# Graph attention behind an expert layer: where the head weights are made ready, and node terms as columns of the head products

## The chip, the cores and the metric

The kernel runs on one core of a Trainium2 chip. The metric is the device time of one execution in microseconds, from start to end, with the median over several executions. The kernel is a long chain of eight layers that hand one 256x768 feature matrix to each other; this text looks at the seam between the sixth (experts, called L2 ffn) and the seventh (graph attention, called L3 gnn).

## The reference

Before the seam comes a mixture of eight experts with top-2 routing, plus one shared expert. Behind it, after a layer norm, stands this graph attention with 12 heads of 64 features (here for 256 nodes and 4096 edges):

```
hv  = h.reshape(n, 12, 64)
ft  = einsum('nhd,od->nho', hv, W)              # one 64x64 weight for all heads
a1  = sum(ft * attn_l, -1);  a2 = sum(ft * attn_r, -1)      # two terms per node and head
e   = leaky_relu(a1[src] + a2[dst], 0.2)
w   = exp(e - segment_max(e, dst)[dst])
agg = segment_sum(w / segment_sum(w, dst)[dst] * ft[src], dst)
res = einsum('nhd,od->nho', hv, W_res)
out = relu(agg + res)
```

A last attention layer with low-rank experts (L3 ffn) follows.

## The kernel before

The 256 rows are two chunks of 128 partitions (`NC = 2`), and the 768 features are six slices of 128 (`KD = 6`). A feature-major copy `xT` of the normed input (`turn_chunk`, line 171 transposes on TensorE, line 172 copies on ScalarE) feeds the products.

**Order of work.** Engines run their queues in order. A planner decides at build time in which order instructions stand in each queue, by modelled costs and dependences; it may move a load or a vector operation far ahead of its place in the text. Instructions wrapped in `pin` keep the order of the text among themselves on their engine. Tiles come from pools with a fixed number of buffers; a new tile of a name waits until the oldest one's readers are done.

**L2 ffn (pools `f2`, `f2a`).** After the router and two thirds of the shared expert, six expert tiles of 128 routed rows are worked off (`for u, parts in enumerate(TILES2)`, line 1695). For each, `pick` (line 1193, VectorE) prepares a one-hot, `take` gathers the rows of a tile ahead with an indirect DMA on the GpSimd queue (line 1120, tile `xg`, buffers `rows`, four of them), `up_tile` and `down_tile` multiply (line 1153), `gated` (lines 1651 to 1657, VectorE) forms the activation, and the result goes to DRAM from the ScalarE queue (line 1210). Weights are streamed by the SP queue through a ring of eight buffers. After the last tile, `add_rows` gathers four times 128 rows back (`yg`, also in the `rows` buffers) and adds them (line 1169); `end_tiles` adds the last products (line 1370) and norms each chunk into `xn` (lines 150 to 160).

**L3 gnn (pools `g3`, `g3a`).** The head weight `W` stands twice on the diagonal of a 128x128 tile, so that one product serves two heads; `bd` holds this for `W` and for `W_res`. It is cleared on VectorE (line 1726), and four DMAs of the ScalarE queue fill its diagonal blocks (line 1729). From `bd` and the two attention rows, VectorE forms `own` (lines 1738 and 1740): `W` applied to the attention vectors, four columns for each pair of heads. Then:

- line 1748: 24 small products `ps_a2 = xT . own`, four columns wide, and line 1751 copies them into `a2`, the node terms `a1` and `a2` of the reference;
- line 1767 (`spread`): products with one column of `own` as broadcast weight, which put a source term on all partitions;
- line 1761 (`piece`): the head products `ft` and `res`, six slices for each of the two chunks, copied out by ScalarE (line 1763). There are four such pieces; two ride behind each of the first two spreads;
- `gat`: for each pair of heads and each chunk, in a software pipeline, `leaky` (line 298 on ScalarE with `a2` as bias, line 299 on VectorE), the row maximum (line 305), the exponentials (line 311), the counted sums (line 318), a transpose (line 326) and the weighted sum (line 338). All of it is pinned.

Attention rows are loaded by `row`, on the GpSimd queue, into a pool of five; the planner issues these loads early (the two of this layer at 999.3 and 1006.8 us). The tile tagged `wide` is a single buffer of 2048 floats per partition, used in turn for `xn` and for the one-hots `hot` of `find` (line 1099). `cnt1` is a mask of the second graph layer; its first half is used again for `mixT` in the expert layers.

Of the kernel before, what the change touches and what calls it, by code (L numbers as in the profile page):

```python
# [8 lines left out]
F32 = mybir.dt.float32  # L9
# [4 lines left out]
OP = mybir.AluOpType  # L14
AX = mybir.AxisListType
# [3 lines left out]
P = 128  # L19
N = 256  # L20
NC = 2
D = 768
KD = D // P
# [30 lines left out]
def graph_ffn_stack_kernel(ctx: ExitStack, tc: tile.TileContext, a: dict, out: bass.AP):  # L54
    nc = tc.nc
# [21 lines left out]
    def acc2(name="acc"):  # L77
        return psacc.tile([P, 2, 512], F32, tag="acc", name=name)
# [18 lines left out]
    pin = tc.keep_in_program_order  # L97
# [16 lines left out]
    def halves(t):  # L114
        return t.rearrange("p (a n) -> p a n", a=2)
# [320 lines left out]
    with tc.tile_pool(name="g0", bufs=1) as g0, tc.tile_pool(name="g0t", bufs=2) as g0t, \  # L436
# [35 lines left out]
        pieces = [(r, c, i) for r in range(NREL) for c in range(NC) for i in range(2)]  # L472

        with tc.tile_pool(name="graph", bufs=1) as gp, tc.tile_pool(name="onehot", bufs=5) as oh:
# [14 lines left out]
            for e in range(NE // P):  # L489
# [31 lines left out]
            ps = bank("ps_cnt").rearrange("p (d n) -> p d n", d=NC)  # L521
# [190 lines left out]
        for layer in range(2):  # L712
# [114 lines left out]
    def wide(name):  # L827
        return masks.tile([P, 2048], F32, tag="wide", name=name)
# [4 lines left out]
    def row(name):  # L833
        src = a[name]
        t = rows.tile([P, 1024], F32, tag="row", name="row")[:, :src.shape[0]]
        nc.gpsimd.dma_start(t, src.partition_broadcast(P))
        return t
# [350 lines left out]
    def pick(pool, is_e, parts):  # L1188

        t = pool.tile([72, P], BF16, name="own")  # L1190
        at = 0
        for r, _, n in parts:
            nc.vector.tensor_copy(t[:, at:at + n], is_e[:, r:r + 1].to_broadcast([72, n]))
            at += n
        return t
# [335 lines left out]
            ready=lambda h: dots(g2a, a2, xl2, 1, 1, D, (asrc, adst), (0,)))  # L1531


    with tc.tile_pool(name="f2", bufs=1) as f2, tc.tile_pool(name="f2a", bufs=2) as f2a:
        table = held.tile([N, D], F32, name="table2")
        nc.gpsimd.dma_start(table.rearrange("(c p) d -> p c d", p=P), xn)
# [76 lines left out]
        more = plan(TILES2)[3]  # L1613

        def gathered(name):
            return f2a.tile([P, D], F32, tag="rows", name=name, bufs=4)

        ys = results[1]

# [72 lines left out]
        cwT = weights_t(f2, cw, 9, "cwT2")  # L1692
        xgT = tile_t(f2a, xg, "xgT")
        last = None
        for u, parts in enumerate(TILES2):
            own, now = pick(f2a, is_e, parts), xgT
            if u < end:
                xg = take(slots[:, u + 1:u + 2])
            acc = acc2("up1_acc")
            up_tile(acc, now, parts, 0, own, range(6), u)  # L1700
            h = first_factor(acc)
            if last is not None:
                gT = turned(f2a, last)
            if u < end:
                xgT = tile_t(f2a, xg, "xgT")
            acc = acc2("up3_acc")
            up_tile(acc, now, parts, 1, own, range(3), u)
            if last is not None:
                finish(f2a, ys[u - 1], gT, views(TILES2[u - 1], "2"), TILES2[u - 1])
                free(u - 1, "2")  # L1710
            up_tile(acc, now, parts, 1, own, range(3, 6), u)
            last = gated(acc, h)
# [9 lines left out]


    with tc.tile_pool(name="g3", bufs=1) as g3, tc.tile_pool(name="g3a", bufs=2) as g3a:
        bd = g3.tile([P, 2, P], F32, name="bd")
        nc.vector.memset(bd, 0.0)
        for i, n in enumerate(("L3_gnn_WT", "L3_gnn_WresT")):
            for j in range(2):
                nc.scalar.dma_start(bd[j * 64:(j + 1) * 64, i, j * 64:(j + 1) * 64], a[n])

        own = g3.tile([P, KD, 2, 2], F32, name="own3")
        nc.vector.memset(own, 0.0)
        for i, n in enumerate(("L3_gnn_attn_l", "L3_gnn_attn_r")):
            r = row(n)
            for j in range(2):
                js = slice(j * 64, (j + 1) * 64)
                t = g3a.tile([P, KD, 64], F32, name="of_row")
                nc.vector.tensor_tensor(t[js], r.rearrange("p (k j o) -> p j k o", k=KD, j=2)[js, j],
                                        bd[js, 0, None, js].to_broadcast([64, KD, 64]), OP.mult)
                nc.vector.tensor_reduce(own[js, :, i, j], t[js], AX.X, OP.add)  # L1740
        xT = g3.tile([P, KD, N], F32, name="xT5")
        for c in range(NC):
            turn_chunk(xn, xT, KD, c)
        a2 = st([P, 2, NC, 12], "gat_a12")
        ps = bank("ps_a2")
        for c in range(NC):
            for k in range(KD):
                nc.tensor.matmul(ps[:, c * 24 + k * 4:c * 24 + k * 4 + 4], xT[:, k, c * P:(c + 1) * P],
                                 own[:, k].rearrange("p w j -> p (w j)"), start=True, stop=True)
        for w in range(2):  # L1750
            nc.vector.tensor_copy(a2[:, w].rearrange("p c (k j) -> p c k j", k=KD),
                                  ps[:, :48].rearrange("p (c k w j) -> p w c k j", c=NC, k=KD, w=2)[:, w])
        ft = g3.tile([P, NC, D], F32, name="ft")
        res = g3.tile([P, NC, D], F32, name="res")
        pieces = [(i, c) for i in range(2) for c in range(NC)]

        def piece():
            i, c = pieces.pop(0)
            acc = acc2("ft_acc")
            for k in range(KD):  # L1760
                pin(nc.tensor.matmul(acc[:, k // 3, (k % 3) * P:(k % 3 + 1) * P], xT[:, k, c * P:(c + 1) * P],  # L1761
                                     bd[:, i, :], start=True, stop=True))
            pin(nc.scalar.copy(halves((ft, res)[i][:, c, :]), acc[:, :, :384]))

        def spread(h, w, ps):
            for j in range(w):
                pin(nc.tensor.matmul(ps[:, j, :], own[:, h // 2, 0, j:j + 1].to_broadcast([P, P]), xT[:, h // 2, :],
                                     start=True, stop=True))
            for _ in range(2 if pieces else 0):
                piece()  # L1770

        h = g3.tile([P, NC, D], F32, name="h5")
        last_xn = normed()

        def post(d, hs, acc, rs):
            scaled(h, acc, rs, 64, 12, hs, d, res[:, d, :])
            s = slice(hs[0] * 64, (hs[-1] + 1) * 64)
            nc.vector.scalar_tensor_tensor(x[:, d, s], h[:, d, s], 0.0, x[:, d, s], op0=OP.max, op1=OP.add)
            if hs[-1] == 11:
                norm(x, last_xn, D, d)  # L1780

        gat(g3a, ft, 12, 64, a2, cnt, neg, OP.max, post, True, spread=spread)
        xn = last_xn

# [134 lines left out]
```

## Time and profile before

| | |
|---|---|
| three runs | 1452.01, 1454.04, 1456.68 us, median 1454.04 us |
| the profiled execution | 1456.74 us, span 1455.0 us |
| TensorE busy | 1259.4 us (87%), mean granted clock 0.916 |
| VectorE, ScalarE, GpSimd busy | 670.2, 477.0, 356.3 us |
| the expert tiles of L2 ffn | about 1107 to 1233 us of the span |
| end of L2 ffn, norm | about 1233 to 1258.6 us |
| L3 gnn up to the pipeline's second leaky | about 1257.9 to 1282 us |
| L3 gnn, rest | about 1282 to 1333 us |
| L3 ffn | from there to 1455 us |

The stage windows of a profile give busy time for each engine in a stretch of the span, and behind it the clock granted to TensorE (1.00 is full speed), the busy share of the DMA engines and what they moved. The chain of waits follows the end of the program back: each line is a start, a duration and the engine and line that held the chain for that time; "ACTq" is ScalarE's queue issuing DMAs, and "issue" is time for which the profile names no wait. A record of a product in this trace is one pass; a product in single precision has two.

### The profile page before, as it was taken

What the parts mean: (1) busy time and instruction counts of PE and PEld (TensorE: products, weight loads), DVE (VectorE), ACT (ScalarE), POOL (GpSimd) and SP (SyncE); (2) the same over time, 40 slices, a digit from 0 to 9 for tenths busy, and PEclk for the clock granted to TensorE, in tenths of its full rate; (3) what the DMA queues carried; (4) which work ended last, traced back from release to release, by engine and by line L of the source; (5) the groups of instructions that cost most, each with busy time, mean ns of one, the idle gap of its engine ahead of it and who ended that gap; (6) DMA issues with size and microseconds to landing.
All of it is one profiled execution on the core that took longest, in us unless ns stands there. A gap on an engine that the chain in (4) does not pass through costs nothing. (4 is left out here: it accounts for less than half of the span.)

```text
span 1455.0 us, 13968 instructions
## 1 busy us (share of the span) xinstructions
PE 1259.4 (87%) x5081; PEld 775.6 (53%) x5102; DVE 670.2 (46%) x1273; ACT 477.0 (33%) x825; POOL 356.3 (24%) x194
## 2 busy tenths in 40 slices
PE   7999999789997874998989859866889999777998
PEld 4576444347643432854545445435576554466854
DVE  4421999930099996164352530067351011455023
ACT  1013877611287662241231122215221111163122
POOL 1001999800099991000203010111001000100000
PEclk9999999989999995999999969987989999775989
DMA  9323250215230023223732149922018998600000
GB/s 332 130 94 102 59 160 6 98 33 195 101 95 0 3 95 115 89 111 143 259 116 76 66 171 389 335 89 73 22 72 342 364 383 334 264 1 33 33 0 22
DMA packets 77689, 196.74 MB, mean 135 GB/s; under 512 B 9036, under 2 KB 23952, under 8 KB 77488
## 3 DMA queue, kind: packets, MB, share of 16 engines
q1 hardware_dynamic: 69088, 162.28, 31.2%
q0 software_dynamic: 6352, 28.33, 5.5%
q10 hardware_dynamic: 2176, 5.18, 1.0%
q8 instruction: 43, 0.70, 0.2%
q14 instruction: 30, 0.25, 0.1%
HBM read 177.45 MB, written 14.87 MB: 132 GB/s over the span
## 5 line engine op out<-in xcount | busy, mean ns | idle before, releaser
L784 POOL TENSOR_TENSOR gate<-gate,qT 128x2048 f32<-128x2048 f32 x64 | 287.8, 4535 | 242.4 <-ACT gate L764 242.0
L769 DVE TENSOR_REDUCE qiT<-gate 128x32 f32<-128x2048 f32 x96 | 215.0, 2279 | 16.2 <-POOL gate L784 15.2
L764 ACT ACTIVATE gate<-gate_acc,bg 128x1024 f32<-128x1024 f32 x192 | 209.8, 1114 | 38.1 <-PE gate_acc L760 35.5
L759 PE MATMUL gate_acc<-sela,ga 128*128 128x512 bf16 x363 | 139.2, 384 | 25.3 <-ACT gate L764 24.8
L760 PE MATMUL gate_acc<-selb,gb 112*128 112x512 bf16 x384 | 147.8, 385 | 1.2
L1153 PE MATMUL up_acc<-w_e,xgT 128*64 128x384 f32 (+1 forms) x432 | 96.4, 489 | 0.0
L760 PEld LDWEIGHTS <-gb 112*128 112x128 bf16 x384 | 37.6, 98 | 96.4 <-issue 71.5
L791 DVE TENSOR_TENSOR gate<-gate,ps_qy 128x2048 f32<-128x2048 f32 x32 | 72.9, 2278 | 0.2 <-ACT gate L764 0.2
L1153 PEld LDWEIGHTS up_acc<-w_e,xgT 128*64 128x64 f32 (+1 forms) x432 | 46.9, 154 | 44.7 <-issue 27.3
L759 PEld LDWEIGHTS <-ga 128*128 128x128 bf16 x384 | 37.8, 98 | 47.8 <-issue 2.2
L642 PE MATMUL ps_alpha<-w_qb,qiT 128*128 128x384 f32 x96 | 44.1, 553 | 19.8 <-DVE qiT L769 19.8
L566 DVE TENSOR_TENSOR ps_hg<-ps_hg,hg 128x384 f32<-128x384 f32 x8 | 4.5, 563 | 107.9 <-ACT hg L565 107.9
L326 PE MATMUL ps_pt<-ident,gat_z 128*128 128x128 f32 x104 | 23.8, 366 | 33.6 <-DVE gat_s L318 33.5
L1120 POOL DMA_INDIRECT yg<-ys,rows x8 | 7.6, 953 | 177.3 <-DMA w_a<-in_L_ffn_AT 118.6
L171 PE MATMUL ps_tr<-ident,xn 128*128 128x128 f32 x84 | 17.7, 380 | 35.4 <-DVE xn L160 20.3
L267 DVE CUSTOM_DVE_ANT_0 gat_dot<-xl,row 128x128 f32<-128x128 f32 (+2 forms) x56 | 23.8, 425 | 52.8 <-ACT xl L1520 19.6
L457 PE MATMUL ps_z<-w_rel,xT 128*128 128x384 f32 x144 | 47.9, 486 | 0.0
L457 PE MATMUL ps_z<-w_rel,nT 128*128 128x384 f32 x144 | 47.7, 491 | 0.0
L461 ACT COPY z<-ps_z 128x384 f32<-128x384 f32 x24 | 11.5, 479 | 105.0 <-PE ps_z L457 105.0
L1651 DVE TENSOR_TENSOR h<-up_acc,h 128x768 f32<-128x768 f32 x6 | 5.7, 958 | 80.1 <-PE up_acc L1153 80.1
L627 PE MATMUL ps_alpha<-w_qa,gT 128*128 128x384 f32 x96 | 40.1, 499 | 0.0
L338 PE MATMUL gat_acc<-xl,gat_pt 128*128 128x128 f32 (+2 forms) x128 | 34.9, 431 | 5.3 <-DVE gat_s L347 5.3
(444 smaller groups left out, 2192.7 us busy)
## 6 DMA issues: line engine op xcount, KB each, us to landing
w_e<-in_L_ffn_W SPq DMA_DIRECT2D x32, 1152.0 KB, 12.2
w_rel<-in_L_gnn_W_rel SPq DMA_DIRECT2D x12, 1152.0 KB, 8.3
wi<-in_L_ffn_WiT SPq DMA_DIRECT2D x8, 1152.0 KB, 15.0
wo<-in_L_ffn_WoT SPq DMA_DIRECT2D x8, 1152.0 KB, 15.5
w_down<-in_L_ffn_W SPq DMA_DIRECT2D x8, 1152.0 KB, 12.2
w_root<-in_L_gnn_W_root SPq DMA_DIRECT2D x4, 1152.0 KB, 11.1
w_ga<-in_L_gnn_WgAT SPq DMA_DIRECT2D x4, 1152.0 KB, 6.4
w_qa<-in_L_gnn_WqAT SPq DMA_DIRECT2D x4, 1152.0 KB, 5.7
```

The source lines that it names most:

```text
L267: pin(nc.vector.tensor_tensor_reduce(t, xl[:, c, h * C:(h + 1) * C], r[:, h * C:(h + 1) * C], 1.0, 0.0, OP.mult, OP.add, accum_out=a2[:, w ...
L338: pin(nc.tensor.matmul(accs[d][:, i, at:at + wide], pts[h, d][:, j, s, :], xl[:, s, lo:lo + wide], start=s == 0, stop=s == NC - 1))
L457: mm = nc.tensor.matmul(ps, hT[:, k, c * P:(c + 1) * P], w(k, i * 384, (i + 1) * 384), start=k == 0, stop=k == KD - 1)
L627: pin(nc.tensor.matmul(al_ps[c][i], hT[:, k, c * P:(c + 1) * P], w(k, i * 384, (i + 1) * 384), start=k == 0, stop=False))
L642: pin(nc.tensor.matmul(al_ps[c][i], qiT[:, f, c * P:(c + 1) * P], w(f, i * 384, (i + 1) * 384), start=False, stop=f == KD - 1))
L759: pin(nc.tensor.matmul(acc[:, i, :], ga[:, b, fs], sela, start=True, stop=False))
L760: pin(nc.tensor.matmul(acc[:, i, :], gb[0:112, u, b, fs], selb[0:112, i], start=False, stop=True))
L764: pin(nc.scalar.activation(g[:, u * 16:(u + 1) * 16, :].rearrange("p n l -> p (n l)"), acc.rearrange("p a n -> p (a n)"), AF.Sigmoid, bias ...
L769: pin(nc.vector.tensor_reduce(qiT[:, f, b * NPB:(b + 1) * NPB], g, AX.X, OP.add))
L784: pin(nc.gpsimd.tensor_tensor(g, g, q[:, None, :].to_broadcast([P, NPB, LQ]), OP.mult))
L791: pin(nc.vector.tensor_tensor(g, g, q_ps[:, None, :].to_broadcast([P, NPB, LQ]), OP.mult))
L1153: pin(nc.tensor.matmul(ps[at:at + n, :], xT[:, k, at:at + n], ws[r](k, lo, hi), start=start, stop=stop))
```

## The change

The head weights are made ready inside the expert layer, and the node terms come out of the head products.

- A tile `heads3` (128 x 6 x 132) in a pool of its own holds for each slice the doubled `W` on the diagonal (128 columns) and behind it the four columns that were `own`. `res3`, the doubled `W_res`, lies in the second half of `cnt1`.
- Before expert tile 1, the GpSimd queue clears both tiles and loads the diagonal blocks (`diagonal`): two DMAs into `heads3`, each of 64 partitions and six runs of 256 bytes, and two into `res3`. Before tile 2, VectorE forms the four columns (`rows_of_heads`), with `wide` as scratch. These instructions are not pinned.
- The buffers `rows` go from four to three.
- In L3 gnn, `heads_of(c)` multiplies a chunk with all 132 columns per slice; two vector copies take the node terms out of PSUM, one scalar copy the 128 others. `heads_of(0)` stands before the pipeline; `heads_of(1)` and `residual_of(0)` follow the first spread, `residual_of(1)` the second.

```diff
+    heads3 = ctx.enter_context(tc.tile_pool(name="late", bufs=1)).tile([P, KD, P + 4], F32, name="heads3")
+    def diagonal(t, name):
+        for j in range(2):
+            js = slice(j * 64, (j + 1) * 64)
+            if len(t.shape) == 3:
+                nc.gpsimd.dma_start(t[js, :, js], a[name][:, None, :].to_broadcast([64, t.shape[1], 64]))
+            else:
+                nc.gpsimd.dma_start(t[js, js], a[name])
+    def rows_of_heads():
+        for i, n in enumerate(("L3_gnn_attn_l", "L3_gnn_attn_r")):
+            r = row(n)
+            for j in range(2):
+                js = slice(j * 64, (j + 1) * 64)
+                t = wide("of_row")[:, :KD * 64].rearrange("p (k o) -> p k o", k=KD)
+                nc.vector.tensor_tensor(t[js], r.rearrange("p (k j o) -> p j k o", k=KD, j=2)[js, j], heads3[js, :, js], OP.mult)
+                nc.vector.tensor_reduce(heads3[js, :, P + 2 * i + j], t[js], AX.X, OP.add)
...
-            return f2a.tile([P, D], F32, tag="rows", name=name, bufs=4)
+            return f2a.tile([P, D], F32, tag="rows", name=name, bufs=3)
...
+        res3 = cnt1[:, 1, :P]
         for u, parts in enumerate(TILES2):
+            if u == 1:
+                for t, n in ((heads3, "L3_gnn_WT"), (res3, "L3_gnn_WresT")):
+                    nc.gpsimd.memset(t, 0.0)
+                    diagonal(t, n)
+            elif u == 2:
+                rows_of_heads()
...
-        bd = g3.tile([P, 2, P], F32, name="bd")
-        nc.vector.memset(bd, 0.0)
...
-                nc.scalar.dma_start(bd[j * 64:(j + 1) * 64, i, j * 64:(j + 1) * 64], a[n])
-        own = g3.tile([P, KD, 2, 2], F32, name="own3")
...
-        for c in range(NC):
-            for k in range(KD):
-                nc.tensor.matmul(ps[:, c * 24 + k * 4:c * 24 + k * 4 + 4], xT[:, k, c * P:(c + 1) * P],
-                                 own[:, k].rearrange("p w j -> p (w j)"), start=True, stop=True)
...
+        def heads_of(c):
             acc = acc2("ft_acc")
             for k in range(KD):
+                pin(nc.tensor.matmul(acc[:, k // 3, (k % 3) * (P + 4):(k % 3 + 1) * (P + 4)], xT[:, k, c * P:(c + 1) * P],
+                                     heads3[:, k, :], start=True, stop=True))
+            v = acc[:, :, :3 * (P + 4)].rearrange("p i (k f) -> p i k f", k=3)
+            for w in range(2):
+                pin(nc.vector.tensor_copy(a2[:, w, c, :].rearrange("p (i k j) -> p i k j", i=2, k=3),
+                                          v[:, :, :, P + 2 * w:P + 2 * w + 2]))
+            pin(nc.scalar.copy(ft[:, c, :].rearrange("p (i k f) -> p i k f", i=2, k=3), v[:, :, :, :P]))
...
+        heads_of(0)
+        pieces = [(heads_of, 1), (residual_of, 0), (residual_of, 1)]
```

More of the change, by code (lines that the diff above doesn't have):

```diff
@@ L1724, in graph_ffn_stack_kernel @@
     with tc.tile_pool(name="g3", bufs=1) as g3, tc.tile_pool(name="g3a", bufs=2) as g3a:
-        bd = g3.tile([P, 2, P], F32, name="bd")
-        nc.vector.memset(bd, 0.0)
-        for i, n in enumerate(("L3_gnn_WT", "L3_gnn_WresT")):
-            for j in range(2):
-                nc.scalar.dma_start(bd[j * 64:(j + 1) * 64, i, j * 64:(j + 1) * 64], a[n])
-        own = g3.tile([P, KD, 2, 2], F32, name="own3")
[L1732 to L1740, printed above, removed]
         xT = g3.tile([P, KD, N], F32, name="xT5")
@@ L1744, in graph_ffn_stack_kernel @@
         a2 = st([P, 2, NC, 12], "gat_a12")
-        ps = bank("ps_a2")
-        for c in range(NC):
-            for k in range(KD):
-                nc.tensor.matmul(ps[:, c * 24 + k * 4:c * 24 + k * 4 + 4], xT[:, k, c * P:(c + 1) * P],
-                                 own[:, k].rearrange("p w j -> p (w j)"), start=True, stop=True)
-        for w in range(2):
-            nc.vector.tensor_copy(a2[:, w].rearrange("p c (k j) -> p c k j", k=KD),
-                                  ps[:, :48].rearrange("p (c k w j) -> p w c k j", c=NC, k=KD, w=2)[:, w])
@@ L1753, in graph_ffn_stack_kernel @@
         ft = g3.tile([P, NC, D], F32, name="ft")
         res = g3.tile([P, NC, D], F32, name="res")
-        pieces = [(i, c) for i in range(2) for c in range(NC)]
-        def piece():
-            i, c = pieces.pop(0)
+        def heads_of(c):
             acc = acc2("ft_acc")
             for k in range(KD):
+                pin(nc.tensor.matmul(acc[:, k // 3, (k % 3) * (P + 4):(k % 3 + 1) * (P + 4)], xT[:, k, c * P:(c + 1) * P],
[5 more added lines that the diff above has]
+            pin(nc.scalar.copy(ft[:, c, :].rearrange("p (i k f) -> p i k f", i=2, k=3), v[:, :, :, :P]))
@@ L1761, in piece, with residual_of @@
+        def residual_of(c):
+            acc = acc2("res_acc")
+            for k in range(KD):
                 pin(nc.tensor.matmul(acc[:, k // 3, (k % 3) * P:(k % 3 + 1) * P], xT[:, k, c * P:(c + 1) * P],
-                                     bd[:, i, :], start=True, stop=True))
-            pin(nc.scalar.copy(halves((ft, res)[i][:, c, :]), acc[:, :, :384]))
+                                     res3, start=True, stop=True))
+            pin(nc.scalar.copy(halves(res[:, c, :]), acc[:, :, :384]))
@@ L1765, in spread @@
+        heads_of(0)
+        pieces = [(heads_of, 1), (residual_of, 0), (residual_of, 1)]
         def spread(h, w, ps):
             for j in range(w):
-                pin(nc.tensor.matmul(ps[:, j, :], own[:, h // 2, 0, j:j + 1].to_broadcast([P, P]), xT[:, h // 2, :],
+                pin(nc.tensor.matmul(ps[:, j, :], heads3[:, h // 2, P + j:P + j + 1].to_broadcast([P, P]), xT[:, h // 2, :],
                                      start=True, stop=True))
             for _ in range(2 if pieces else 0):
-                piece()
+                if pieces:
+                    of, c = pieces.pop(0)
+                    of(c)
```

## The prediction

> **What bounds the kernel now.** I read three views: the stage windows, to see which engine is full where; then the chain of waits over the seam; then the timeline there, for durations and for what sits idle. The windows for an expert-tile stretch, the seam and the start of the graph layer (columns: stretch, length, busy time with count for TensorE, its weight loads, VectorE, ScalarE, GpSimd; then granted clock, DMA share, GB/s):
>
> ```profile
> 1130.00:1160.00 30.00, 30.00 (x140) 15.84 (x136) 3.22 (x8) 5.38 (x11) 0.00 (x0) 1.00 1.01 389
> 1253.00:1267.00 14.00, 4.06 (x17) 2.94 (x16) 9.88 (x22) 2.23 (x6) 0.00 (x0) 0.68 0.57 217
> 1267.00:1282.00 15.00, 13.67 (x79) 13.02 (x79) 0.96 (x3) 4.43 (x8) 0.00 (x0) 0.73 0.01 1
> ```
>
> Among the tiles TensorE is full, VectorE is idle nine tenths of the time and GpSimd does nothing. At the seam it is the reverse: TensorE works 4 of 14 us, VectorE 9.9. The chain of waits says what for:
>
> ```profile
> 1257.94 0.53 ACTq L1729
> ...
> 1260.46 1.65 ACT xT L172 x4
> 1262.10 4.48 issue
> 1266.59 5.25 PE ps_a L1748 x24
> 1271.84 1.91 PE ps_row L1767 x4
> 1273.75 3.38 PE ft_acc L1761 x24
> 1277.13 0.87 PE ps_row L1767 x4
> 1277.99 2.69 PE ft_acc L1761 x24
> 1280.71 0.80 ACT res L1763
> 1281.51 0.74 ACT gat_z L298 x2
> ```
>
> ScalarE issues four DMAs before it may copy `xT`. The 4.48 us of "issue" have no name here; the timeline gives it:
>
> ```profile
> 1261.86 1.14 DVE L1738 TENSOR_TENSOR of_row<-row,bd 64x384 f32<-64x384 f32 x2 [3.27 <-DMA bd<-in_L_gnn_WT]
> 1265.35 1.13 DVE L1740 TENSOR_REDUCE own<-of_row 64x6 f32<-64x384 f32 x2
> 1266.59 5.25 PE L1748 MATMUL ps_a<-own,xT 128*128 128x4 f32 x24 [6.02 <-issue]
> ```
>
> VectorE waits for the DMA, makes `own` until 1266.5, and TensorE then spends 5.25 us on products four columns wide. The last copy (1280.71) is the event to follow: ScalarE's queue puts the second leaky behind it, and the pipeline only starts then.
>
> **The change, part by part.**
>
> *Preparation removed from the seam.* TensorE ends its 12 transposes at 1260.57 (1257.86 + 2.71). The two copies of chunk 0 no longer wait behind four DMA issues (2.5 us) and run under the transposes, at 0.41 us each. So `heads_of(0)`, which needs only chunk 0, can start at 1260.6, where `ps_a2` started at 1266.59. The two clears of VectorE inside the norm (0.27 and 0.08 us) go as well; they stood before the second chunk's statistics, and I count 0.3 us.
>
> *Products.* New order on TensorE: head piece, spread, head piece, residual piece, spread, residual piece. A piece is 12 records. At full clock the trace has 24 in 2.84 us, so 1.42 a piece; at half clock I solve 24 in 3.58 us with the clock rising at 1275.1 for about 0.24 us a record, 2.9 a piece. A spread costs 1.9 us at half clock, 0.95 at full (chain: 1.91 and 0.87). Four more columns on 128 add 3%, under 0.1 us a piece. The sum turns on when the clock rises. The trace: after the restart at 1266.59 it stood at 0.50 until about 1275.1, 8.5 us, more than half of this in the narrow products; after the restart at 1287.0 it stood at 0.50 until about 1292.1, 5.1 us. The Trainium skill, "TensorE: Matmul & The Clock Gate", Part 1, says that about 3.4 us of sustained work bring full rate. From 1260.6:
>
> - rule (full at 1264.0): pieces and spreads end about 1270.1;
> - 5.1 us (full at 1265.7): 3.0 + 1.9 + 1.5 + 1.42 + 0.95 + 1.42 give 1270.8;
> - 8.5 us (full at 1269.1): 3.0 + 1.9 + 3.0 + 1.7 + 1.0 + 1.42 give 1272.6.
>
> Before, they ended at 1280.68. Gain 10.6, 9.9 or 8.1 us. The restart without narrow products is nearer, but one row is little, so I take 9.5. ScalarE's copies (0.80 each) fit between the pieces, and an accumulator is free again before its next piece: of two, the first is copied at 1263.7 to 1264.5, and residual 0 starts after 1266. The first leaky now stands behind three copies where it stood behind two; it still runs before the second, which decides. VectorE takes four node-term copies for two, 0.18 us each, while ScalarE copies.
>
> *VectorE among the tiles.* Four products and four sums, 2.28 + 2.26 = 4.5 us, move there. VectorE has 3.2 us of work in 30. What queues behind them is `gated`, ended at 1149.79 for tile 1 and read by TensorE's transpose only at about 1155, so 5 us of cover each tile; and `pick`, two tiles ahead. Cost 0. Without that cover it would be 1:1 on a full TensorE, up to 4.5 us plus any wait for the diagonal; that is the second rival.
>
> *GpSimd's queue.* Two clears (0.74 for `zero`, 128x768; 0.24 for 128x128) and four DMA issues (0.53 to 1.08 us on this queue) make 3 to 5.3 us. Behind them may stand gathers `xg`, each fetched a tile ahead. GpSimd is idle from 1118 to 1236.7, so 0. The data: 2 x 98 KB + 2 x 16 KB = 229 KB, 0.6 us of DMA at 389 GB/s. Against the change speaks the skill's "DMA: Bandwidth & Descriptors", Specifications: pieces under 512 bytes fall short of line rate, and these runs have 256. By that I double it, an estimate of 1.2 us. TensorE waits for a weight in this stage only at 1234.93 (2.36 us, for the shared expert), and the ring refills as TensorE frees it, so a delay at 1120 should be gone by then: 0, at worst 1.2, not below 0 as bytes are only added.
>
> *Three gather buffers.* `xg` for tile 3 is issued when tile 0 is read (1107.9), tiles 4 and 5 at about 1117 and 1134; they are used at 1155, 1177 and 1198. The margins exceed 40 us: 0. The last gather of `yg` now waits until VectorE has added the first, at 1244.3 where it went at 1240.5. From issue to add the four took 6.6 to 7.5 us, so it is added from 1251.1 to 1252.0 and ends by 1253.0; the add behind it (line 1370) starts at 1252.68, held by TensorE. Cost 0 to 0.4 us, I take 0.3.
>
> *Sum.* 9.5 + 0.3 - 0.3 = 9.5 us. All of it reaches the end if the rest moves along: the last layer's first weights had landed by 1262, when the DMA share falls to 0. Its later loads, `bl` (issued 1333.5, used 1353.8, lands in 4.9 us) and the second half of `w_p`, hang on readers that move as well. The profiled execution took 1456.74 us (span 1455.0), so it would take 1447.2; the median of the runs shown is 2.7 us lower, and I predict from it: 1454.0 - 9.5 = **1444.5 us**.
>
> **The rivals.**
>
> 1. *The forecast*, about 1441 to 1449 us. Chance 0.61.
>
> 2. *VectorE blocks on the diagonal before the first tile; slower.* The eight operations are not pinned. `wide` comes free at 1094.6, and VectorE is idle from 1094.8 to 1106.7; the planner may put them there. Then they wait for `heads3`, and behind them stands line 1555, which frees the PSUM bank of the gather's transposes for a full TensorE. The hole fits 4.5 us, so it costs 1 us for each us that the diagonal lands after 1102.2. Three gathers end on GpSimd at 1099.2; with the clear and two issues it is 1101.1. By the fit of the same DMA page (Anatomy of one DMA: 2.0 us + bytes / 436 GB/s) it would be there at about 1103.4 and cost 1 us. The nearest row is the gather on this queue beside the weight stream, 7.5 us: 1108.6, cost 6.4 us, time 1451. From 1111.7 on the whole gain is gone, from 1116 it is slower by over 0.3%: 15 us for the DMA, as long as the 3 MB of `ys<-zero` took. For it: 768 short runs in a share of 0.77. Against it: the planner issued the attention rows 250 us ahead and may clear and load `heads3` as early. Time 1449 to 1462, chance 0.22, over half of it slower in the end.
>
> 3. *The clock stays low.* If TensorE runs the whole restart at half rate, as it did behind the last layer's restart at 1334 for 10 us and more, four pieces and two spreads take 4 x 2.9 + 2 x 1.9 = 15.4 us and end at 1276: gain 4.7, 1449.3 us. Narrow router products stood in that stretch, and here only full ones. Chance 0.09.
>
> 4. *It does not do what it says.* The planner's new order costs elsewhere in unpinned work (the last layer interleaves value products with the router by its choice) about what the seam gives, or the copies of chunk 0 stay late for another reason. Time 1450 to 1458, chance 0.08.
>
> **How the numbers follow.** About 0.3%, 4.4 us, is what a measurement of this kernel can tell from no change. Faster by more, under 1449.7: all of 1, a sixth of 2, two thirds of 3, a quarter of 4, 0.61 + 0.04 + 0.06 + 0.02 = 0.73. Within: 0.06 + 0.03 + 0.03 = 0.12. Slower: 0.12 + 0.03 = 0.15. The range goes from the fastest case (10.6 + 0.3 us of gain, and the 2 us by which the fastest run lies below the median: 1441) to 1456, which leaves out about 1 in 10 above and 1 in 10 below or at its lower edge.
>
> **What would show it.** Right: no ScalarE DMA issues at the seam; the first head record about 3.5 us after that norm's start; no group of 24 four-column products; the last residual copy about 14 us after the first norm of `xn` (line 160), where it came 23.6 us after it (1257.12 to 1280.71); clock 0.50 for less than 9 us there; of_row and its sums among the tiles, with TensorE still at 30.00 of 30. Wrong: a wait of VectorE's of_row on a DMA with TensorE's ps_xg idle behind it; the line 1169 adds ending after 1254; head pieces that start more than 5 us after that norm; or a seam shorter by 9 us with the time given back behind 1333.

## The result, and the profile after

The changed kernel takes 1442.47 us in the median of four runs (1440.01 to 1442.73), beside 1454.42 us for the kernel before (1452.01 to 1456.68): a ratio of 0.9914, 95% interval 0.9895 to 0.9934. It is faster by 12.0 us, where 9.5 were forecast. The profiled execution took 1442.42 us (span 1440.7, mean granted clock 0.920).

First the stage windows of the changed kernel, with the columns of before: an expert-tile stretch and the seam.

```profile
1132.57:1162.57 30.00, 30.00 (x136) 15.59 (x136) 3.22 (x8) 4.99 (x11) 0.95 (x1) 1.00 1.03 398
1251.00:1265.00 14.00, 10.29 (x64) 9.33 (x64) 5.75 (x16) 5.35 (x11) 0.00 (x0) 0.88 0.55 211
```

The tiles are as full as before (30.00 of 30). At the seam TensorE now works 10.29 us of 14 where it worked 4.06. The chain of waits of the changed kernel over the seam:

```profile
1254.93 0.69 DVE xn L160
...
1255.67 2.67 PE ps_tr L171 x12
1258.34 1.88 PE ft_acc L1762 x12
1260.21 0.86 PE ps_row L1782 x4
1261.08 1.35 PE ft_acc L1762 x12
...
1266.01 0.80 ACT res L1775
```

No ScalarE DMA, no "issue" of more than 0.05 us, no narrow products: TensorE goes from the transposes to the head products without a gap. From the first norm (line 160) to the last residual copy it is 11.08 us, where it was 23.59 (1257.12 to 1280.71). That is a gain of 12.5 us at one place. From that copy to the end of the span it is 174.69 us after and 174.29 before, so in this pair of profiles nothing is given back.

The other thing to see is in TensorE's windows of one us (stretch, length, busy time, granted clock, DMA share, GB/s), again of the changed kernel:

```profile
1255.00:1256.00 1.00, 0.33 (x2) 0.94 1.02 393
1256.00:1257.00 1.00, 1.00 (x6) 0.50 1.03 399
...
1259.00:1260.00 1.00, 1.00 (x9) 0.86 0.00 0
1260.00:1261.00 1.00, 1.00 (x7) 1.00 0.00 0
```

A row between 1.00 and 0.50 places the change inside it. A mean of 0.94 puts the fall 0.88 us into its row, at 1255.88; a mean of 0.86 puts the rise 0.28 us into its row, at 1259.28. The difference is 3.40 us. The same reading of the kernel before:

```profile
1258.00:1259.00 1.00, 1.00 (x6) 0.51 1.02 396
...
1275.00:1276.00 1.00, 1.00 (x11) 0.96 0.00 0
```

It falls at 1258.02 and rises at 1275.08, 17.06 us or five times 3.41 later. Read in this way, the 44 changes of the clock that one such row shows singly in the profile of before, and the 48 of after, lie within 0.04 us of multiples of 3.4135 us, from the first to the last; only the offset differs from one execution to the next (1.87 us into the period, counted from the span's start, and 3.13). The Trainium skill, "TensorE: Matmul & The Clock Gate", Part 1 (What's actually happening), states such a window, 3413 ns, running free of the program; the traces show that length. So the clock changes only on a grid that the program does not set. What TensorE must have done in a window for the clock to rise or fall at its end is what the experiments ask.

### The profile page after: what moved, and what is told of

Read it like the earlier page. It is cut to its first block, busy times and chain, and to the rows that moved or that the text cites. A ratio compares the mean times of both kernels' runs of the same rounds, so it can differ in the third digit from the quotient of the medians.

```text
span 1440.7 us, 13924 instructions
## 1 busy us (share of the span) xinstructions
PE 1251.3 (87%) x5057; PEld 769.4 (53%) x5078; DVE 669.9 (46%) x1273; ACT 476.8 (33%) x825; POOL 359.8 (25%) x200
## 5 line engine op out<-in xcount | busy, mean ns | idle before, releaser
L1120 POOL DMA_INDIRECT xg<-table,slots x12 | 11.7, 977 | 108.9 <-DVE of_row L1550 35.9
```

## The experiments

Two theories stand in the expectations. **C**: the seam's length is set by the removed work and also by the clock's windows, whose outcome turns on how full each was of wide products (products of many columns, where the narrow ones have four); and where the grid falls is chance. **W**: the removed work alone counts, and the clock follows from the order of the work. To compare profiles that start a little differently, I measure each from the first add of line 1370 to the start of the last residual copy ("seam"), and from there to the end of the span ("tail"). Each ratio is to the kernel before measured beside that run, where its median was 1454.42 (after), 1456.64 (prep_only to late_diagonal), 1456.91 (after_again to warm_both) and 1456.95 us (the last four); medians of different groups are better compared by their ratios.

| kernel | median us | ratio to before, 95% | seam us | tail us |
|---|---|---|---|---|
| before | (profile: span 1455.0) | 1 | 28.03 | 174.29 |
| after | 1442.47 | 0.9914 [0.9895, 0.9934] | 15.31 | 174.69 |
| prep_only | 1449.01 | 0.9944 [0.9926, 0.9963] | 21.24 | 174.45 |
| cols_only | 1445.43 | 0.9926 [0.9899, 0.9954] | 20.19 | 168.58 |
| act_dmas | 1445.45 | 0.9928 [0.9909, 0.9947] | 17.80 | 174.27 |
| late_diagonal | 1443.67 | 0.9908 [0.9887, 0.9929] | 15.07 | 169.27 |
| after_again | 1443.49 | 0.9905 [0.9878, 0.9932] | 15.31 | 174.68 |
| warm_seam | 1435.53 | 0.9867 [0.9825, 0.9909] | 13.79 | 167.84 |
| warm_last | 1435.28 | 0.9847 [0.9817, 0.9877] | 15.30 | 165.20 |
| warm_both | 1429.00 | 0.9804 [0.9777, 0.9831] | 13.79 | 163.60 |
| before_warm | 1443.46 | 0.9913 [0.9895, 0.9931] | 24.83 | 163.11 |
| rows_x8_warm | 1432.70 | 0.9836 [0.9814, 0.9857] | 13.79 | 163.67 |
| late_diagonal_warm | 1438.18 | 0.9871 [0.9851, 0.9890] | 13.79 | 163.40 |
| warm_three | 1432.38 | 0.9840 [0.9821, 0.9860] | 13.79 | 164.85 |

### The preparation moved, but the node terms as narrow products again (prep_only)

```diff
-        heads_of(0)
-        pieces = [(heads_of, 1), (residual_of, 0), (residual_of, 1)]
+        ps = bank("ps_a2")
+        for c in range(NC):
+            for k in range(KD):
+                nc.tensor.matmul(ps[:, c * 24 + k * 4:c * 24 + k * 4 + 4], xT[:, k, c * P:(c + 1) * P],
+                                 heads3[:, k, P:P + 4], start=True, stop=True)
...
+        pieces = [(i, c) for i in range(2) for c in range(NC)]
```

> Preparation moved as in the changed kernel, but the node terms come from 24 four-column products at the seam, and the head pieces have 128 columns in the old order. Theory W (the gain is the removed work alone): 5.3 us slower than the changed kernel, the price of ps_a2 in the trace of before, so about 7 us under the kernel before. Theory C (the TensorE clock rises only at the end of a 3.4 us window that full-width products fill; four-column products do not fill one): the granted clock stays at 0.50 through the narrow products and some 3 us of full ones behind them; the last residual copy comes about 6 us later after the first norm of xn than in the changed kernel (17.2 us where it is 11.1), about 6 us under the kernel before.

TensorE's timeline at the seam of prep_only, and its windows there:

```profile
1260.80 5.12 PE L1762 MATMUL ps_a<-heads,xT 128*128 128x4 f32 x24
1265.79 2.05 PE L1779 MATMUL ps_row<-xT,heads 128*128 128x256 f32 x4
```

```profile
1262.00:1264.00 2.00, 2.00 (x11) 0.50 0.00 0
...
1268.00:1269.00 1.00, 1.00 (x8) 0.67 0.02 8
```

The clock falls at 1258.42 and rises at 1268.66, three windows. The middle one, 1261.8 to 1265.2, holds narrow products back to back with TensorE busy for all of it, and the clock stays at 0.50 behind it. The first, 1258.4 to 1261.8, is the closest pair to the changed kernel: the same transposes at the same place in the window, followed for its last us by narrow products where the changed kernel has head products. Its clock stayed low and that of the changed kernel rose. It rises here only after a window that is mostly spreads and head products. So "busy" in the profile's sense is not what the window asks for: here four-column products did not raise the clock. The median does not choose between the theories (7.6 us under before, where W had about 7 and C about 6); the profile does. From first norm to last copy it is 17.01 us, 5.9 more than after: most of it the narrow products' 5.12 us, the rest mostly spreads and head products that still ran at half clock behind them.

### The columns, but VectorE's sums at the seam (cols_only)

```diff
-                    diagonal(t, n)
-            elif u == 2:
-                rows_of_heads()
...
+        for t, n in ((heads3, "L3_gnn_WT"), (res3, "L3_gnn_WresT")):
+            diagonal(t, n)
+        rows_of_heads(g3a)
```

with the diagonal's loads on ScalarE's queue again.

> Node terms as columns of the head products, but the diagonal blocks are loaded at the seam by four DMAs of the ScalarE queue, and VectorE makes the four columns there (clears moved ahead). Theory W: the head products start some 6.3 us later than in the changed kernel and everything behind moves with them, so about 6 us slower than it and 6 us under the kernel before. Theory C: the same start, but the clock has to be raised again from the restart, first at a window's end behind one window of full products; some 8 to 9 us slower than the changed kernel, 3 to 4 us under the kernel before. The two parts alone would then sum to less than both together.

Both expectations missed the total: it is 11.2 us under before, where W had 6 and C 3 to 4. The timeline says why for the seam:

```profile
1254.83 0.50 DVE L1550 TENSOR_TENSOR of_row<-row,heads 64x384 f32<-64x384 f32 x1
...
1260.63 1.13 DVE L1551 TENSOR_REDUCE heads<-of_row 64x6 f32<-64x384 f32 x2
1261.97 2.98 PE L1762 MATMUL ft_acc<-heads,xT 128*128 128x132 f32 x12 [0.75 <-ACT xT L172]
```

`heads3` lies in a pool that is open from early on, so the planner issued its loads at 1055.7 us, and VectorE's sums threaded themselves into the norm. The kernel is thus "sums at the seam" and not "sums and loads at the seam". The sums still cost: the norm starts 5.58 us after the first add (1251.93 to 1257.51) where after took 4.23, the last sum ends at 1261.8, and the clock is low for three windows. The seam is 4.9 us longer than after. But the tail is 6.1 us shorter, though the edit changes no work there: in the last layer the clock came back at 1329.1 us, 57 us after the last copy, and in after at 1334.4, 68 us after it.

### ScalarE's four DMAs put back (act_dmas)

```diff
+        bd = g3.tile([P, 2, P], F32, name="bd")
+        for i, n in enumerate(("L3_gnn_WT", "L3_gnn_WresT")):
+            for j in range(2):
+                nc.scalar.dma_start(bd[j * 64:(j + 1) * 64, i, j * 64:(j + 1) * 64], a[n])
```

> The changed kernel with four more DMAs issued by ScalarE at the seam, into a tile that nothing reads: the four issues of the kernel before alone, without anyone waiting for the data. By the prediction's step the copies of xT wait for 2.4 us of issues: head pieces start about 1 us later (they need chunk 0 only), 1 to 2 us slower than the changed kernel by theory W. Theory C: a later start can miss a window, 1 to 4 us. If the issues cost nothing, 0 us.

ScalarE's timeline, its queue's DMA issues included:

```profile
1248.46 1.17 ACTq L1755 DMA_DIRECT2D bd<-in_L_gnn_WT  x2
1249.67 1.25 ACTq L1755 DMA_DIRECT2D bd<-in_L_gnn_WresT  x2
1250.95 1.28 ACT L152 ACT_TABLE_LOAD   x1 [4.83 <-DMA w_v<-in_L_ffn_W_qkvT]
```

Nothing reads these loads, so the planner let them go ahead of the norm instead of behind it, and there they hold up the table load and the root that the norm waits for: 5.65 us from the first add to the norm (1247.13 to 1252.78) in place of 4.23. The rest of the seam's 2.5 us is one more window at half clock (it fell at 1252.36 and rose at 1259.18). In both kernels what stood behind the issues in ScalarE's queue waited for them: here the norm, in before the copies of `xT`. This is read from the profile: the median is 2 to 3 us above the changed kernel's by the ratios (W had 1 to 2, C 1 to 4), but the intervals overlap.

### The second rival, made to happen (late_diagonal)

```diff
-                    nc.gpsimd.memset(t, 0.0)
-                    diagonal(t, n)
+                late = st([P, 1], "late_zero")
+                nc.vector.tensor_scalar(late, slots[:, 2:3], 0.0, None, op0=OP.mult)
...
+                nc.gpsimd.tensor_tensor(heads3[:, 0, :], heads3[:, 0, :], late.to_broadcast([P, P + 4]), OP.mult)
...
+                diagonal(heads3, "L3_gnn_WT")
+                diagonal(res3, "L3_gnn_WresT")
```

> The changed kernel with the load of the diagonal into heads3 held back until the gather indices of the tiles are known (GpSimd's multiply by a zero made from them), so that its two DMAs go out behind three gathers, at about 1098 us; the planner leaves four of_row products and three sums in front of line 1575 on VectorE. Prediction's second rival: VectorE waits for the landing and TensorE loses 1 us for each us past its hole; with 7.5 us to landing as the gathers took, 5 to 6 us slower than the changed kernel; with 2.2 us, under 0.5 us. If the expert tiles cover it in any case: 0.

```profile
1099.20 1.46 POOL L1540 DMA_DIRECT2D heads<-in_L_gnn_WT  x2
...
1106.90 0.55 DVE L1550 TENSOR_TENSOR of_row<-row,heads 64x384 f32<-64x384 f32 x1 [12.58 <-DMA heads<-in_L_gnn_WT]
...
1111.93 0.90 PE L1128 MATMUL ps_xg<-ident,xg 128*128 128x128 f32 x3 [5.25 <-DVE hsw L1575]
```

This is the stall that the prediction drew: VectorE stands on the load beside the weight stream (7.7 us from issue), the PSUM bank comes free late, and a TensorE that was full stands for 5.25 us. Yet the total does not show it: the ratio is that of the changed kernel within the intervals. Its tail is 5.4 us shorter than after's; the clock was low in the attention of the last layer for four windows (1397.2 to 1410.9) and in after for six (1392.4 to 1412.9). In that one profile, then, the clock elsewhere made up for the local loss. So the clock had to be held before small costs could be read.

### The clock held by filler products (after_again, warm_seam, warm_last, warm_both)

All are the changed kernel; after_again has no edit. The fillers are 256 columns wide, write a PSUM bank that nobody reads, and stand where TensorE is idle. warm_seam has seven ahead of the transposes of `xT5`:

```diff
+        def dense(n, rhs):
+            ps = one_bank("qy", "dense")
+            for _ in range(n):
+                pin(nc.tensor.matmul(ps[:, :256], ones, rhs, start=True, stop=True))
+        dense(7, cnt[:, 0, :])
         xT = g3.tile([P, KD, N], F32, name="xT5")
```

warm_last has four ahead of each chunk's transposes at the start of the last layer, and warm_both has both edits:

```diff
-        for c in range(NC):
-            turn_chunk(xn, xT, KD, c)
+        dense(4, cnt[:, 0, :])
+        turn_chunk(xn, xT, KD, 0)
+        dense(4, xn[:, 0, :256])
+        turn_chunk(xn, xT, KD, 1)
```

> The changed kernel as it is, once more, beside the three fillers. Both theories: 0.991 of the kernel before, 1441 to 1446 us. Theory C (the granted clock follows windows of about 3.41 us that run free of the program, each judged by how full TensorE was of wide products): in the new profile the clock changes fall at other offsets from the first norm of the last layer, so the seam from that norm to the last residual copy need not be 11.08 us again, but 11 to 14 us, and the clock at the start of the last layer may rise up to 12 us earlier or later than the 68 us after that copy seen before. Rival W (the clock depends on the order of the work alone): 11.1 us and 68 us again, within 0.5 us.

> The changed kernel with seven products of 256 columns, whose result nobody reads, put into TensorE's idle 3.7 us ahead of the transposes at the seam. Theory C: the clock is still 1.00 through most of the transposes, which then take 1.6 to 2.0 us in place of 2.67, and the first six head products 1.4 us in place of 1.88; from the first norm to the last residual copy 9.7 to 10.5 us in place of 11.08; total 0.5 to 1.5 us less than the changed kernel. Rival W (the clock falls because of the stall before it, by the order of the work): the same as without the fillers, or up to 0.5 us slower where they end after the first norm.

> The changed kernel with eight products of 256 columns, whose result nobody reads, in TensorE's two idle stretches at the start of the last attention layer (four ahead of each chunk's transposes; the stretches were 2.3 and 2.1 us, a product takes about 0.55 us at half clock). Theory C: the clock rises between 1317 and 1325 us instead of at 1334.2; the 14 to 16 us of back-to-back work at 0.50 shrink by 3 to 6 us, and so does the total. Rival W (the rise needs the wide products of the attention scores themselves): no earlier rise, and 0 to 2 us slower by the fillers.

> The changed kernel with the fillers of both places. Theory C: the sum of the two, 4 to 7 us less than the changed kernel, 1436 to 1440 us on a chip where that takes 1443. Rival W: 0 to 2.5 us more than the changed kernel.

The changed kernel again gave the same seam and the same tail (15.31 and 174.68 us). In this W's numbers were met, and C's chance was not seen. The windows of after_again show why:

```profile
1256.00:1257.00 1.00, 0.52 (x3) 0.85 1.03 399
1260.00:1261.00 1.00, 1.00 (x10) 0.95 0.00 0
```

The clock falls 0.96 us behind the first norm (1255.74), and in after it fell 0.95 us behind it, in before 0.90 and in prep_only 0.88, though the norm came at times up to 2.6 us apart. So at the seam these four executions stood at nearly the same place of the grid. The program falls into step with the grid as it runs. Measured by the starts of its products on TensorE, the 14 profiles were spread over 2.6 us of the 3.41 at 10 us, and thirteen of them stood within 0.07 us at 1069 us. Between after and after_again the difference went from 0.82 us at 10 us to 0.41 at 16 and 0.20 at 301 (later, timing that differs between executions can drive two profiles apart again for a while, to 1.59 us at 1098). A stretch at half clock that ends on a grid line would do this, since a start later by some time then ends later by half of it; that is worked out from the clocks of 0.50 and 1.00, and no run tests it.

Whether the clock matters at all is decided by the fillers. The chain of waits of warm_seam:

```profile
1257.41 0.69 DVE xn L160
...
1258.14 1.66 PE ps_tr L171 x12
1259.80 1.37 PE ft_acc L1768 x12
```

The transposes take 1.66 us where they took 2.67, the first head piece 1.37 where it took 1.88, with the clock at 1.00 throughout: 9.55 us from norm to last copy (9.56 in one), in every changed kernel with this filler, against 11.08. In the last layer, windows of TensorE in the changed kernel, then in warm_both:

```profile
1322.00:1324.00 2.00, 2.00 (x12) 0.50 0.18 68
```

```profile
1322.00:1324.00 2.00, 2.00 (x15) 0.97 0.42 175
```

TensorE is full in both rows; without filler it runs at half speed until 1334.4, through router products eight columns wide, and with filler it is at full speed from 1322.1. The two together reach 1429.0 us, 0.9804 [0.9777, 0.9831] of the kernel before and faster than the changed kernel alone, 0.9905 [0.9878, 0.9932] on the same chip. In warm_last alone the clock rose at 1325.8, 51.6 us after the last copy. C's sign is right, and W, which had no gain from fillers, fell. But C's sizes were too small: against after_again, warm_seam gained 8.0 us in the median where 0.5 to 1.5 were expected, warm_last 8.2 for 3 to 6, both together 14.5 for 4 to 7. Of these the sum is clear of the noise and warm_last just so; the interval of warm_seam overlaps that of after_again, and for it the 1.5 us at the seam, read in the profile, is what is sure.

### What the work was worth at a held clock, and the covers again (before_warm, rows_x8_warm, late_diagonal_warm, warm_three)

before_warm is the kernel before with `dense(7, ...)` ahead of its transposes and `dense(12, ...)` ahead of its narrow products. The other three are warm_both with one edit each. late_diagonal_warm has that of late_diagonal; rows_x8_warm makes the row sums twice for each of four tiles, with the rows kept from the first time:

```diff
-            elif u == 2:
+            for _ in range(2 if u >= 2 else 0):
                 rows_of_heads()
```

and warm_three puts `dense(7, xT[:, 0, :])` behind the first two `weigh` of the last attention:

```diff
         ahead = [weigh(0), weigh(1)]
+        if fill:
+            fill()
         for hp in range(KD):
```

> The kernel before, with products of 256 columns, whose result nobody reads, in TensorE's two idle stretches at the seam: seven ahead of the transposes (idle 3.9 us) and twelve ahead of the narrow node-term products (idle 6.0 us). It tells what of the 12.5 us that the change gained at the seam is work taken away and what is the granted clock. Theory C: the clock stays 1.00 to the node-term products, which still start 9.5 us after the first norm (VectorE's sums release them); from the norm to the last residual copy 9.5 + 24 x 0.107 + 2 x 0.86 + 4 x 1.35 = 19.2 us in place of 23.6 (up to 21 where the narrow products let the clock fall behind them), total 2.5 to 4.5 us less than the kernel before, ratio 0.997 to 0.998; the work taken away is then 19.2 less 9.55 = 9.6 us, and the clock's share the rest. Rival W (the clock is the same by the order of the work): 23.6 us at the seam and the time before.

> The changed kernel with both fillers, and with VectorE's products and sums of the attention rows among the second layer's tiles done eight times in place of once (31 us more of VectorE work; the rows are loaded once). Cover theory (the prediction's: this work lies in VectorE's idle time beside TensorE-bound tiles): within 1.5 us of the kernel with both fillers alone, 0.980 to 0.982 of the kernel before. Rival (VectorE's queue has no such slack, and the single copy hides only by luck of its place): 5 to 31 us more, 0.984 to 1.002.

> The changed kernel with both fillers, and with the clears and loads of the block diagonals held back until the third tile's slots are there, as in the run without fillers, where TensorE then stood 5.25 us behind the products of the rows. There the total did not show it. Theory C: those 5 us were lost where they were seen, and the granted clock's phase in the last layer gave them back in some executions; with the clock held by the fillers the total is 4 to 6 us above the kernel with both fillers alone, 0.983 to 0.985 of the kernel before. Rival (the loss is taken up again by slack behind it, whatever the clock): within 1 us of it, 0.980 to 0.981.

> Both fillers, and a third: seven products of 256 columns in the last layer's attention, where TensorE waits 3.2 us for the first softmax and the clock fell to 0.50 for some 20 us in the changed kernel (1393 to 1412 us), but not in the profile with both fillers. Theory C: that place was a matter of phase too, so the third filler gains nothing where the clock stays up anyway and up to 7 us in executions where it would fall: median 0 to 2 us less than with both fillers, 0.979 to 0.981, and a narrower spread. Rival (the first fillers already settle it): 0 to 1 us more, by products that end after the softmax.

The chain of waits of before_warm:

```profile
1259.22 4.80 DMA bd<-in_L_gnn_WT
...
1268.12 0.56 DVE own L1740
...
1268.72 2.84 PE ps_a L1755 x24
```

With the clock held the narrow products take 2.84 us, not 5.25, and the seam 24.83 us, not 28.03. (From norm to last copy 20.39 us; 19.2 were expected, and the rest is mostly that the narrow products started 10.3 us after the norm, not 9.5, as the load took 4.80 us to land.) So of the seam's 12.7 us, 24.83 - 13.79 = 11.0 are work and waits taken away, and 1.7 the clock: before lost 3.2 us to it, after 1.5. The slower load is in the 11.0; with the one of before (3.92 us from the same issue to the first product of line 1738) it would be an estimated 10.1, and the clock's share 2.6.

The covers, the idle time that hides moved work, can now be read. In rows_x8_warm and in late_diagonal_warm, TensorE's wait ahead of the first tile's next gather transposes:

```profile
1108.46 0.55 PE L1128 MATMUL ps_xg<-ident,xg 128*128 128x128 f32 x3 [0.27 <-DVE hsw L1577]
```

```profile
1112.55 0.90 PE L1128 MATMUL ps_xg<-ident,xg 128*128 128x128 f32 x3 [5.43 <-DVE hsw L1575]
```

Eight times the row work, which ran from 1095 to 1139 us, well into the tiles (TensorE's first gather transposes stood at 1107.7), leaves this wait where warm_both has it (0.28 us), and on one chip 1432.70 us stand beside the 1432.38 of warm_three; the ratio 0.9836 lies a little over the band expected from warm_both, which was timed on another chip and whose interval overlaps. The late diagonal makes TensorE wait 5.43 us there, and costs 5.5 to 5.8 us in the median beside those two, the 4 to 6 us of C, though its ratio, too, lies over the band expected; the intervals overlap a little (0.9851 to 0.9890, and 0.9821 to 0.9860), so the trace carries this more than the ratio. The third filler gains nothing that can be told.

## Why the prediction held, point by point

The mechanism was right, and the gain at the seam was forecast 3 us too small, mostly by one term. That the rest of the kernel took the same time before and after was in part luck: the prediction did not price the clock behind the seam, and other runs have tails down to 163 us.

- *Preparation removed from the seam*: right. The head products started 3.4 us after the first norm (1254.93 to 1258.34); 3.5 were forecast, as chunk 0's copies ran under the transposes. cols_only and act_dmas price its parts: sums in the norm and loads in ScalarE's queue each make the norm 1.4 us late, apart from what follows.
- *Products*: right in kind; a piece took 1.35 us at full clock (1.42 forecast) and a spread 0.86 (0.95).
- *When the clock rises* is the term of the sum that was mis-sized. The prediction counted from the first head product, and weighed 3.4, 5.1 or 8.5 us of restart. The clock rose 0.94 us after the head products began, as the window that ended at 1259.28 had been filled by the transposes and that 0.94 us together. TensorE had been busy without a gap since the first transpose (1255.67), 3.61 us before the rise; so the about 3.4 us of sustained work in the Trainium skill, "TensorE: Matmul & The Clock Gate", Part 1 (What's actually happening), come near the measured 3.61 if they are counted from there, and not from the head products. The grid gives the prediction's two examples too: the restart of 5.1 us (1287.0) came 1.7 us into a window (1285.3 to 1288.7), and the clock rose at the end of the next; that of 8.5 us had narrow products in its first full window. The last residual copy was forecast about 14 us after the first norm and came 11.08 us after it; all of the seam was forecast at 9.5 us and gave 12.5.
- *VectorE among the tiles*, cost 0: right, shown by eight times the work at no visible cost. In the changed kernel itself the sums stood ahead of the tiles (below).
- *GpSimd's queue and the bytes*, cost 0: right. TensorE waited 2.41 us for the shared expert's weights, 2.36 before.
- *Three gather buffers*, 0.3 us: nothing seen. The last gather was issued at 1242.62 and added from 1249.18, ahead of the adds of line 1370 at 1250.70.
- *The second rival* was a true danger, and the changed kernel escaped it by what the planner did with one load. The timeline of the changed kernel:

```profile
1054.48 1.35 POOL L1540 DMA_DIRECT2D heads<-in_L_gnn_WT  x2 [0.30 <-POOL heads L1719]
...
1092.82 0.55 DVE L1550 TENSOR_TENSOR of_row<-row,heads 64x384 f32<-64x384 f32 x1
...
1104.68 0.88 DVE L1575 SCALAR_TENSOR_TENSOR hsw<-ps_e,cols,hsw 128x256 f32<-128x256 f32 x2 [7.21 <-PE ps_e L102]
```

  The sums stand in just the hole that it named, ahead of line 1575 (1555 before), but the load had gone out 38 us earlier; the prediction had named this chance, without counting on it. Forced late, it cost 5.25 to 5.43 us; the prediction had 6.4 for a landing of 7.5.
- *The third rival* (clock low all through) fell: one window. *The fourth* fell: the tail is the same to 0.4 us. The profiled executions differ by 14.3 us, and 2.0 of these lie ahead of the first add (1252.68 and 1250.70), in a part that the change hardly touches. The same point came at 1251.51 in the second profile of the changed kernel, and between 1247.13 and 1253.31 in the other kernels without fillers and without the late diagonal, so 2.0 us are within what executions scatter there.

## What to carry to other kernels

Before pricing a restart of TensorE, find the grid: read two changes of the clock off one-us windows and lay a ruler of that spacing over the timeline. Then ask of each window whether it is full of wide products; an idle half window, or a run of narrow products, can cost more than the work in it, and products that nobody reads, put into a stall, can pay. And do not take a local gain or loss of 5 us from totals while the clock downstream can move by several windows: hold the clock first, then compare.

## What the runs showed of the hardware that was not expected

- The clock's changes lie on a grid of 3.4135 us to within 0.04 us over a whole span, at another offset in each execution. TensorE full of four-column products for a window did not raise it (1261.8 to 1265.2 us in prep_only). In the 14 profiles every rise stood behind a window in which TensorE was busy for at least 0.8; the reverse does not hold.
- A stretch can keep the clock that it is entered with. The attention of the last layer, in the changed kernel and then in warm_both:

```profile
1396.00:1400.00 4.00, 4.00 (x18) 0.50 0.00 0
```

```profile
1396.00:1400.00 4.00, 3.64 (x22) 1.00 0.00 0
```

  In after the clock fell at 1392.4, behind 2.2 us of waiting for the first softmax, and stayed low for six windows with TensorE full. Most of the time there goes to products on half of the array (forms 64*128 and 128*64 in the groups), which may be why; no run tests it.
- Fillers at the seam shortened the tail as well, 140 us later. In the eight profiles without them that attention stretch was low for three to six windows; in the five that have them and no filler of its own, for none or one. That, and a clock that came back sooner in the last layer (58.9 us after the last copy, 69.5 in before), is where most of the gain of before_warm lies (13.5 us in the median, 3.2 at the seam). The traces show what goes with it. The wait for the first softmax was 2.17 us in each of these thirteen, and the number of low windows behind it follows where in its grid window this wait began:

| kernels | wait began, us into its window | windows low |
|---|---|---|
| before, cols_only, act_dmas, prep_only | 0.04 to 0.17 | 5 |
| after, after_again | 0.18 | 6 |
| late_diagonal | 0.59 | 4 |
| warm_last | 0.85 | 3 |
| late_diagonal_warm, before_warm | 1.06, 1.21 | 1 |
| warm_seam | 1.58 | 1 |
| rows_x8_warm, warm_both | 1.68, 1.73 | 0 |

  In after the whole wait lies in one window, busy for 0.36 of it. In the last row a grid line cuts the wait in two: the windows are busy for 0.49 and 0.87 in rows_x8_warm, 0.51 and 0.86 in warm_both, and the clock did not fall. In warm_seam the first was busy for 0.47, and it fell. A filler at the seam moves all that stands behind it, and so moves this wait along the grid; that it helps there was not designed. No run moves this stretch alone, so this is an ordering of thirteen single executions and not a test; why fewer windows are low when the wait begins later in its window is open.
